# Cross-attention of 20 heads on one Trainium2 core: score tiles of 234, 234 and 156 columns instead of 308, 154 and 154, the second high keys loaded by DMA, and a new order of the batch loop

## Chip, cores and metric

The kernel runs on one core of a Trainium2 chip. The metric is the device time of the program in microseconds (us), the median of several runs; lower is better. The core has a matrix engine (TensorE, in the profile PE, its weight loads PEld), a vector engine (VectorE, DVE), an engine for activations (ScalarE, ACT), a general one (GpSimd, POOL), and SyncE (SP), which here only issues DMA transfers. Each engine works through its own instructions in order; semaphores tie them together.

## The reference, cut to what matters

```
B, S, C = (32, 512, 640); CA = 1024; HEADS = 20; HD = 32     # as drawn
q = heads(x @ to_q_w)                          # 20 heads of 32
k = heads(ctx[:, :77] @ to_k_w)                # 77 text tokens per batch
v = heads(ctx[:, :77] @ to_v_w)
p = softmax(q @ k.T / sqrt(32))                # 77 keys
out = merge(p @ v) @ to_out_w + to_out_b + x
```

The context has 77 tokens, so the three further attentions of the reference (objects, others, images) have no keys and add nothing. All is float32.

## The kernel before

**Numbers in two parts.** Each float32 matrix is split into a high part (`float32r`, the form that TensorE takes) and a low part, the rest. A product is made of three: high by high, high by low, low by high.

**Chunks.** Four heads are 128 rows, so a batch has five chunks; chunk `n` stands for batch `n // 5`, heads `4 * (n % 5)` and on. For each chunk:

- `queries` (line 542, the group pq): 15 products of 512 columns.
- `high_query` (ACT), `copy_query` (POOL, line 783), `low_query` (DVE, line 787) make the three stationary sets `qt[:, 0..2]`: set 0 holds the high query of the four heads; the upper half of set 1 and the lower half of set 2 hold copies of it, the other halves the low query.
- `score_tile` (line 577, the group sc), four tiles of 128 queries: one product of set 0 with the keys of all four heads, 308 = 4 x 77 columns, then one of set 1 with the keys of heads 0 and 1 (154 columns), and one of set 2 with those of heads 2 and 3 (154). A head's 32 rows meet only its own columns, since the key tile is zero elsewhere. A tile stands in one of three PSUM buffers.
- `score_max` (DVE), `exps` (ACT, line 602: four exponentials with their sums), `sums` (DVE, line 612), `normalize` (POOL, line 617), `block_transpose` (DVE), `store_p` (line 633): the weights `pn` go turned to DRAM (`pd<-z`).
- three to four chunks later `load_rows` reads them back (`raw<-pd`, lines 648 and 650), ACT, DVE and POOL split them (`pp`; POOL's part is line 679), and `value_pass` (line 694, pa) makes six products of 512 columns.
- `project` (line 750, po) makes the output: 120 products of 320 columns per batch, then a residual, a bias (POOL, line 743) and a store.

POOL also makes the low part of x (line 320).

**Keys.** They are computed at the start for all batches and stand in DRAM (`k_dram`), high and low. The key tile `kb0` serves chunks 0 to 2, `kb1` chunks 3 and 4. For each batch, `load_keys` brings, per head and group, the high keys to the head's own rows (part 0) and the low keys to another head's rows (part 1), and `copy_half_keys` (POOL, line 519) copies the high keys into the block that set 0 uses.

**The order.** A written table sets the order of everything: each token is one step (`s` score tile, `k` copy of the query, `q` queries, `v` value pass, `p` output product, `d` load of the weights, `w` store of the weights, `uk` load of keys, `K` copy of keys, `N` normalise). `FILL` covers the keys, the values and the first two batches, `PLAN` is one batch and is run 29 times, `LAST_` is the end. A token's place fixes the order on each engine, not its time. SP has one queue for loads and stores; each transfer takes one of eight lanes in turn, and waits for the one before it in its lane.

Of the kernel before, what the change touches and what calls it, by code (L numbers as in the profile page):

```python
# [23 lines left out]
P = 128  # L24
Q = 32
HEADS = 20
HD = 32
# [4 lines left out]
NBLK = HPC * KPAD // Q  # L32

# [18 lines left out]
def kernel(  # L52
# [394 lines left out]
    def open_small():  # L447
        nonlocal small
        if small is None:
# [3 lines left out]
            kbs.append(small.tile([P, 4, GROUPS[0][1], KCOLS // 2], FPR, name="kb0"))  # L453
# [9 lines left out]
    def open_second():  # L463
        nonlocal z
        if not vbs:
# [3 lines left out]
            kbs.append(pool.tile([P, 4, GROUPS[1][1], KCOLS // 2], FPR, name="kb1"))  # L469
# [33 lines left out]
    def load_keys(b, g, heads=range(HPC), parts=(0, 1)):  # L503
        j0, nj = GROUPS[g]
        src = k_dram[g][:, :, :, b * NKEY : (b + 1) * NKEY].bitcast(F32)
        kb = kbs[g].bitcast(F32)
        for i in heads:
            own, half = slice(i * HD, (i + 1) * HD), slice(i % 2 * NKEY, (i % 2 + 1) * NKEY)
            other = slice(*((i + 2) % HPC * HD + k for k in (0, HD)))
            for part, rows in enumerate((own, other)):  # L510
                if part in parts:
                    nc.sync.dma_start(kb[rows, 1 + i // 2, :, half], src[own, part])

    def load_head_keys(b, g, i, part):
        load_keys(b, g, (i,), (part,))

    def copy_half_keys(g, h):
        kb, rows = kbs[g], slice(64 * h, 64 * h + 64)
        nc.gpsimd.tensor_copy(kb[rows, 3 * h], kb[rows, 1 + h].bitcast(F32))

    def copy_keys(g):
        copy_half_keys(g, 0)
        copy_half_keys(g, 1)
# [26 lines left out]
    def split_q(n):  # L550

        qt, pq = qts[n % 2], pqs.pop(n)
        nc.scalar.copy(qt[:, 0, :], pq)
        lower, upper = slice(0, 64), slice(64, P)
        halves = ((lower, upper), (upper, lower))
        for w, (r, other) in enumerate(halves):
            nc.gpsimd.tensor_copy(qt[other, 1 + w, :], qt[r, 0, :].bitcast(F32))
        for w, (r, other) in enumerate(halves):
            nc.vector.tensor_tensor(
                qt[r, 1 + w, :], pq[r], qt[r, 0, :].bitcast(F32), ALU.subtract  # L560
            )

    def score_tile(n, t):
        b, j = divmod(n, NC_)
        g = GROUP_OF[j]
        qt, kb = qts[n % 2], kbs[g]
        jg = j - GROUPS[g][0]
# [560 lines left out]
```

## Time and profile before

| | |
|---|---|
| median of 3 runs | 1858.24 us (1858.23 to 1858.27) |
| profiled execution, its span | 1856.5 us, at clock 1.000 |
| PE busy | 1842.4 us (99%) |
| DVE, ACT, POOL busy | 1563.4, 1527.2, 1303.9 us |
| score products, weight-load rows (line 577) | 1920 in 640 tiles |
| copies of the query on POOL (line 783) | 320, 0.615 us each |
| copies of the keys on POOL (line 519) | 128, 0.443 and 0.576 us |
| loads of keys | 512, 28.9 and 19.2 KB |

How to read it: a busy share is that of the time in which at least one instruction of the engine ran. Matmuls overlap their neighbours, so the length of a row in the timeline is more than what a product adds; the distance from one start to the next is what counts. "idle before" names what ended an engine's idle time. The profile's own time is its span; the median is 1.7 us above it.

### The profile page before, as it was taken

The page shows a single profiled execution, that of the slowest core. Times are in us where ns is not written, and L with a number is a line of the kernel's source. Part 1 is how long each engine was busy: PE and PEld are TensorE (multiplying, and loading weights), DVE is VectorE, ACT ScalarE, POOL GpSimd, SP SyncE. Part 2 cuts the span into 40 slices and gives each one's busy share as a digit, 9 for nine tenths or more (in the row PEclk, how much of TensorE's full clock was granted, in tenths as well). Part 3 has the DMA queues.
Part 4 walks back from the last instruction along what each step waited for, and adds up shares of the span by engine and source line. Part 5 has one row for each costly group of instructions (what it writes and reads, how often), then busy time and mean ns, then how long its engine had stood idle before and what let it go on. Part 6 is the DMA issues. An engine that isn't in the chain of part 4 may idle for free.

```text
span 1856.5 us, 37492 instructions
## 1 busy us (share of the span) xinstructions
PE 1842.4 (99%) x10332; PEld 1655.7 (89%) x10332; DVE 1563.4 (84%) x2502; ACT 1527.2 (82%) x6218; POOL 1303.9 (70%) x1120
## 2 busy tenths in 40 slices
PE   9999999999999999999999999999999999999998
PEld 7888897889999999999999999999999999999998
DVE  5445458899999999999999999999999999999996
ACT  3233248899999999999999999999999999999984
POOL 1100268778788788778778877887778878877874
PEclk9999999999999999999999999999999999999999
DMA  9889779998998898888998888998889988888875
GB/s 188 199 198 249 184 193 256 254 242 235 247 240 243 240 238 232 242 235 236 238 244 237 234 243 237 244 238 237 235 234 244 244 241 236 237 232 243 228 228 187
DMA packets 563296, 431.37 MB, mean 232 GB/s; under 512 B 191120, under 2 KB 471120, under 8 KB 563088
## 3 DMA queue, kind: packets, MB, share of 16 engines
q1 hardware_dynamic: 558192, 413.16, 84.5%
q0 software_dynamic: 4800, 15.65, 2.7%
q8 instruction: 85, 1.39, 0.3%
q14 instruction: 123, 1.01, 0.2%
q10 hardware_dynamic: 96, 0.16, 0.0%
HBM read 247.17 MB, written 181.64 MB: 231 GB/s over the span
## 4 chain that ended last, share of the span: by engine, by line
PE 93%; DMA 4%; SPq 1%; DVE 1%; ACT 1%; issue 0%; POOL 0%; DVEq 0%; ACTq 0%; POOLq 0%
PE po L750 29%; PE pq L542 28%; PE pa L694 12%; PE sc L577 11%; PE pv L204 7%; PE pk L204 6%; DMA pd<-z 1%; DMA cs<-in_ctx_dram 1%; DMA xr<-in_x_dram 1%; DMA wo_s<-wo_dram 0%; DMA wraw<-in_L_xattn_to_v_w_dram 0%; DMA xs<-in_x_dram 0%; DMA wraw<-in_L_xattn_to_k_w_dram 0%; ACT pn L602 0%; DMA raw<-pd 0%
## 5 line engine op out<-in xcount | busy, mean ns | idle before, releaser
L602 ACT ACTIVATE pn<-sc,nm 128x77 f32<-128x77 f32 x2560 | 797.1, 343 | 36.0 <-DVE nm L588 29.6
L750 PE MATMUL po<-wo_s,at 128*128 128x320 f32 x3840 | 707.2, 310 | 0.1
L750 PEld LDWEIGHTS po<-wo_s,at 128*128 128x128 f32 x3840 | 619.7, 188 | 41.1 <-DVE xr L765 0.6
L542 PE MATMUL pq<-xt,wq_s 128*128 128x512 f32 x2400 | 596.7, 394 | 2.9 <-ACT pp L661 1.9
L602 ACT ACTIVATION_READ_ACCUMULATOR pn<-sc,nm 128x1 f32 x2560 | 567.5, 222 | 0.0
L542 PEld LDWEIGHTS pq<-xt,wq_s 128*128 128x128 f32 x2400 | 436.7, 188 | 82.5 <-ACT pp L661 2.1
L617 POOL TENSOR_TENSOR pn<-pn,rs 128x1232 f32<-128x1232 f32 x160 | 389.4, 2434 | 94.0 <-DVE rs L612 90.0
L694 PE MATMUL pa<-pp,vb 128*128 128x512 f32 x960 | 340.9, 403 | 4.1 <-DVE at L731 3.3
L577 PEld LDWEIGHTS sc<-kb,qt 128*128 128x128 f32 x1920 | 302.9, 188 | 14.4 <-ACT pn L602 1.8
L588 DVE TENSOR_REDUCE nm<-sc 128x4 f32<-128x308 f32 x640 | 295.0, 466 | 21.6 <-PE sc L577 16.7
L577 PE MATMUL sc<-kb,qt 128*128 128x154 f32 (+1 forms) x1920 | 301.9, 274 | 0.9 <-ACT pn L602 0.9
L783 POOL CAST qt<-qt 64x512 fp32r<-64x512 f32 x320 | 196.9, 615 | 139.5 <-ACT qt L779 124.4
L712 DVE TENSOR_TENSOR pa<-pa,aw 64x512 f32<-64x512 f32 x320 | 222.3, 695 | 50.4 <-ACT aw L708 43.2
L679 POOL TENSOR_TENSOR pp<-raw,pp 64x512 fp32r<-64x512 f32 x160 | 207.0, 1294 | 66.9 <-ACT pp L661 53.5
L624 DVE STREAM_TRANSPOSE z<-pn 128x1280 f32<-128x1280 f32 x160 | 241.2, 1507 | 8.8 <-DMA pd<-z 3.4
L708 ACT COPY aw<-pa 64x1024 f32<-64x1024 f32 x160 | 162.2, 1014 | 85.0 <-PE pa L694 83.9
L787 DVE TENSOR_TENSOR qt<-pq,qt 64x512 fp32r<-64x512 f32 x320 | 216.8, 678 | 13.9 <-ACT qt L779 9.0
L320 POOL TENSOR_TENSOR xt<-xs,xt 128x512 fp32r<-128x512 f32 x160 | 204.6, 1305 | 20.8 <-ACT xt L316 15.8
L743 POOL TENSOR_TENSOR xr<-xr,bias 128x640 f32<-128x640 f32 x128 | 202.3, 1581 | 13.1 <-issue 3.5
L672 DVE TENSOR_TENSOR pp<-raw,pp 128x1024 fp32r<-128x1024 f32 x160 | 195.7, 1223 | 0.0
L694 PEld LDWEIGHTS pa<-pp,vb 128*128 128x128 f32 x960 | 173.8, 189 | 15.1 <-DVE pp L672 2.3
L663 ACT CAST pp<-raw 128x1024 fp32r<-128x1024 f32 x160 | 168.1, 1051 | 0.7 <-DMA raw<-pd 0.7
(46 smaller groups left out, 1584.2 us busy)
## 6 DMA issues: line engine op xcount, KB each, us to landing
pd<-z SPq DMA_DIRECT2D x640, 160.0 KB, 3.4
raw<-pd SPq DMA_DIRECT2D x160, 512.0 KB, 4.5
xr<-in_x_dram SPq DMA_DIRECT2D x128, 320.0 KB, 3.9
out_dram<-xr SPq DMA_DIRECT2D x127, 320.0 KB, 3.7
xs<-in_x_dram SPq DMA_DIRECT2D x124, 320.0 KB, 5.8
raw<-pd SPq DMA_DIRECT2D x160, 128.0 KB, 4.2
v_dram<-vs SPq DMA_DIRECT2D x80, 192.0 KB, 4.0
k_dram<-ks POOLq DMA_DIRECT2D x20, 512.0 KB, 4.2
```

The costliest lines, as they stand in the source:

```text
L204: nc.tensor.matmul(held[j][:, :gn], w[:, k, a, :], cts[g, k][:, c, :gn], start=(k == 0 and n == 0), stop=(k == NK - 1 and n == 2),)
L542: nc.tensor.matmul(pqs[n], wq_s[:, k, a, j * P : (j + 1) * P], xts[b, k][:, c, :], start=(k == 0 and m == 0), stop=(k == NC_ - 1 and m == 2),)
L577: nc.tensor.matmul(sc[:, cols], qt[:, m, t * P : (t + 1) * P], keys_, start=(m == 0), stop=(m == 2),)
L588: nc.vector.tensor_reduce(nm, sc[:, :KCOLS].rearrange("p (h k) -> p h k", k=NKEY), AX.X, ALU.max, negate=True)
L602: nc.scalar.activation(pnb[n % 2][:, at, :NKEY], sc[:, i * NKEY : (i + 1) * NKEY], AF.Exp, bias=nm[:, i : i + 1], accum_out=sms[n][:, at : ...
L617: nc.gpsimd.tensor_tensor(pf, pf, rs.unsqueeze(2).to_broadcast([P, NQ * HPC, NKEY]), ALU.mult)
L624: nc.vector.transpose(z.rearrange("p b t j -> p t b j"), pn.rearrange("p (t h) k -> p t (h k)", t=NQ).rearrange("p t (b i) -> p t b i", i=Q),)
L679: nc.gpsimd.tensor_tensor(pp[64:, 4, :], raw[:64, 2, :], pp[:64, 4, :].bitcast(F32), ALU.subtract)
L694: nc.tensor.matmul(pas[n][:, p, :], vb[:, p, t, :], pp[:, c, :], start=(c == p), stop=(c == p + 2),)
L712: nc.vector.tensor_tensor(pa[64 * p : 64 * p + 64, 0], pa[:64, p], aw[:, p], ALU.add)
L750: nc.tensor.matmul(pos[b, t, h][:, :HALF], ats[b * NC_ + j][:, a, t * P : (t + 1) * P], wos[0][:, j, c, h * HALF : (h + 1) * HALF], start= ...
L787: nc.vector.tensor_tensor(qt[rows, 1 + w, :], pqs[n][rows], qt[rows, 0, :].bitcast(F32), ALU.subtract)
```

## The change

A head's columns are now 78 wide (`KBLK`, 77 keys and one empty), in the order of heads 2, 0, 1, 3. The twelve products of 32 rows that a tile needs (three parts by four heads) are dealt out over the three stationary sets in another way:

- set 0 (heads 2, 0, 1; 234 columns): high queries of heads 0, 1, 2 and, in the last 32 rows, of head 0 a second time, against its low keys.
- set 1 (heads 0, 1, 3; 234 columns): low queries of heads 0 and 1, high queries of heads 1 and 3.
- set 2 (heads 2, 3; 156 columns, in two pieces of the PSUM tile): high and low queries of heads 2 and 3.

The query needs four copies on POOL instead of two, one of 64 rows and three of 32 (`COPIES`). The last one overwrites head 3's high rows in set 0, so it comes after all that reads them. High keys are needed at two places; the second is loaded from DRAM as part 2 of `load_head_keys`, and the copies on POOL and their token `K` are gone. That is 24 key loads per batch instead of 16. The reduction and the exponentials read the same number of elements, with a step of 78.

`PLAN` is a new order of all steps, not the old one with tokens exchanged. In `FILL` and `LAST_` the old order stands: `k0 k1` where `k0` was, `k2 k3` where `k1` was, part 2 behind part 0, and no `K`.

```diff
+KBLK = NKEY + 1
+ORDER = (2, 0, 1, 3)
+KEYS_AT = (0, 3 * KBLK, 6 * KBLK)
+KEYS_OF = (
+    ((0, 0, 1), (0, 3, 1), (1, 0, 0)),
+    ((0, 1, 2), (1, 2, 1), (1, 1, 1)),
+    ((0, 2, 0), (2, 0, 0), (2, 2, 0)),
+    ((1, 3, 2), (2, 1, 1), (2, 3, 1)),
+)
+COPIES = ((2, 0, 64, 64), (1, 96, 96, 32), (1, 64, 32, 32), (0, 96, 0, 32))
...
-            kbs.append(small.tile([P, 4, GROUPS[0][1], KCOLS // 2], FPR, name="kb0"))
+            kbs.append(small.tile([P, GROUPS[0][1], 8 * KBLK], FPR, name="kb0"))
...
     def load_head_keys(b, g, i, part):
-        load_keys(b, g, (i,), (part,))
-
-    def copy_half_keys(g, h):
-        kb, rows = kbs[g], slice(64 * h, 64 * h + 64)
-        nc.gpsimd.tensor_copy(kb[rows, 3 * h], kb[rows, 1 + h].bitcast(F32))
+        src = k_dram[g][i * HD : (i + 1) * HD, part % 2, :, b * NKEY : (b + 1) * NKEY].bitcast(F32)
+        m, quad, block = KEYS_OF[i][part]
+        c0 = KEYS_AT[m] + block * KBLK
+        nc.sync.dma_start(
+            kbs[g].bitcast(F32)[quad * HD : (quad + 1) * HD, :, c0 : c0 + NKEY], src
+        )
...
+    def score_blocks(sc):
+        return sc[:, : HPC * KBLK].rearrange("p (h k) -> p h k", k=KBLK)
+
     def score_tile(n, t):
...
-        half = KCOLS // 2
-        for m, (cols, keys_) in enumerate(
-            (
-                (slice(0, KCOLS), kb[:, 0::3, jg]),
-                (slice(0, half), kb[:, 1, jg]),
-                (slice(half, KCOLS), kb[:, 2, jg]),
-            )
-        ):
+        blocks = score_blocks(sc)
+        for m, heads in enumerate((blocks[:, 0:3], blocks[:, 1:4], blocks[:, 0::3])):
+            nh = (3, 3, 2)[m]
+            keys_ = kb[:, KEYS_AT[m] : KEYS_AT[m] + nh * KBLK].rearrange("p (h k) -> p h k", k=KBLK)
             nc.tensor.matmul(
-                sc[:, cols],
+                heads,
                 qt[:, m, t * P : (t + 1) * P],
                 keys_,
                 start=(m == 0),
                 stop=(m == 2),
+                skip_group_check=True,
             )
...
     def copy_query(n, w):
-        qt, half = qts[n % 2], (slice(0, 64), slice(64, P))
-        nc.gpsimd.tensor_copy(qt[half[1 - w], 1 + w, :], qt[half[w], 0, :].bitcast(F32))
+        qt, (m, r1, r0, rn) = qts[n % 2], COPIES[w]
+        nc.gpsimd.tensor_copy(qt[r1 : r1 + rn, m, :], qt[r0 : r0 + rn, 0, :].bitcast(F32))
...
     PLAN = (
-        "1uv10 0r 0e0 0s2 0ux3 0g0 0N 0v0 1uv15 0v1 0m1 0v2 0f10 0p16 1uv11 0e1 0v4 0g1 0uk120 0p17 0v3 "
+        "1uv13 0uk121 0m1 0e0 0v1 0k0 0g1 0s2 0p16 0v3 0uk122 0f10 0ux3 0v0 0v5 0e1 0v2 0m2 0v4 0r 0uk111 "
...
-        elif op == "K":
-            copy_half_keys(*arg)
```

**Where instructions move.** On TensorE, in the loop, two score tiles of one chunk (sc, output from PSUM's three tiles; kb is the key tile, qt the query) between query (pq), output (po) and value (pa) products. Before:

```order
L694 MATMUL pa<-pp,vb_2005 128x512
L750 MATMUL po<-wo_s,at_2689 128x320 x3
L577 MATMUL sc<-kb_1753,qt_1920 128x308
L577 MATMUL sc<-kb_1753,qt_1920 128x154 x2
L577 MATMUL sc<-kb_1753,qt_1920 128x308
L577 MATMUL sc<-kb_1753,qt_1920 128x154 x2
L542 MATMUL pq<-xt,wq_s 128x512 x15
```

and after the change:

```order
L538 MATMUL pq<-xt,wq_s 128x512 x9
L726 MATMUL po<-wo_s,at_2715 128x320 x3
L558 MATMUL sc<-kb_2007,qt_1923 128x234 x2
L558 MATMUL sc<-kb_2007,qt_1923 128x2x78
L558 MATMUL sc<-kb_2007,qt_1923 128x234 x2
L558 MATMUL sc<-kb_2007,qt_1923 128x2x78
L726 MATMUL po<-wo_s,at_2379 128x320 x3
L670 MATMUL pa<-pp,vb_2009 128x512 x6
```

A tile has three products as before, the longest is shorter, and the two others of 154 are one of 234 and one of two pieces of 78; query products are now cut up between output products.

On POOL, in the loop, the stretch from the normalisation (pn) ahead of the query's copies (qt) for chunk 3 to the copies for chunk 4; pp is POOL's part of the weights, xt the low part of x, xr the bias. Before:

```order
L617 TENSOR_TENSOR pn_1922<-pn_1922,rs 128x16x77
L783 CAST qt_1920<-qt_1920 64x512 x2
L679 TENSOR_TENSOR pp<-raw,pp 64x512
L743 TENSOR_TENSOR xr<-xr,bias 128x640
L617 TENSOR_TENSOR pn_1921<-pn_1921,rs 128x16x77
L679 TENSOR_TENSOR pp<-raw,pp 64x512
L320 TENSOR_TENSOR xt<-xs,xt 128x512
L783 CAST qt_1919<-qt_1919 64x512 x2
L320 TENSOR_TENSOR xt<-xs,xt 128x512 x4
```

and after the change:

```order
L593 TENSOR_TENSOR pn_1924<-pn_1924,rs 128x16x77
L759 CAST qt_1922<-qt_1922 64x512
L759 CAST qt_1922<-qt_1922 32x512 x3
L330 TENSOR_TENSOR xt<-xs,xt 128x512
L719 TENSOR_TENSOR xr<-xr,bias 128x640
L593 TENSOR_TENSOR pn_1925<-pn_1925,rs 128x16x77
L655 TENSOR_TENSOR pp<-raw,pp 64x512
L330 TENSOR_TENSOR xt<-xs,xt 128x512 x4
L759 CAST qt_1923<-qt_1923 64x512
L759 CAST qt_1923<-qt_1923 32x512 x3
```

Two copies became four, and those for chunk 4 moved behind the four splits of x.

On SP, in the loop, stores of the weights (pd) and the load of earlier weights (raw) that follows them, each with what it waits for (DMAHW is one of the eight lanes). Before:

```order
L633 DMA pd<-z 32x10x128 [waits DMAHW4_49,DVE_49]
L512 DMA kb_1753<-k_dram_60 32x3x77 [waits DMAHW5_49]
L633 DMA pd<-z 32x10x128 [waits DMAHW6_49]
L633 DMA pd<-z 32x10x128 [waits DMAHW7_49]
L633 DMA pd<-z 32x10x128 [waits DMAHW0_49]
L739 DMA xr<-in_x_dram 128x640 [waits DMAHW1_49]
L302 DMA xs<-in_x_dram 32x16x160 [waits DMAHW2_49,Pool_49]
L650 DMA raw<-pd 64x512 [waits DMAHW3_49]
L648 DMA raw<-pd 128x2x512 [waits DMAHW4_49,DMAHW0_49,DMAHW6_49,DVE_49,DMAHW7_49,Activation_49,Pool_49]
```

and after the change:

```order
L609 DMA pd<-z 32x10x128 [waits DMAHW7_49,DVE_49]
L609 DMA pd<-z 32x10x128 [waits DMAHW0_49]
L609 DMA pd<-z 32x10x128 [waits DMAHW1_49]
L527 DMA vb_2009<-v_dram 32x3x96 [waits DMAHW2_49]
L624 DMA raw<-pd 128x2x512 [waits DMAHW3_49]
L517 DMA kb_1753<-k_dram_60 32x3x77 [waits DMAHW4_49]
L609 DMA pd<-z 32x10x128 [waits DMAHW5_49]
L517 DMA kb_1753<-k_dram_60 32x3x77 [waits DMAHW6_49]
L312 DMA xs<-in_x_dram 32x16x160 [waits DMAHW7_49,Pool_49]
```

The load of weights waited for the four stores just ahead of it; now it waits for its lane only.

More of the change, by code (lines that the diff above doesn't have):

```diff
@@ L468, in open_second @@
             pool = ctx.enter_context(tc.tile_pool(name="second", bufs=1, reuse_waits="tile"))
-            kbs.append(pool.tile([P, 4, GROUPS[1][1], KCOLS // 2], FPR, name="kb1"))
+            kbs.append(pool.tile([P, GROUPS[1][1], 8 * KBLK], FPR, name="kb1"))
             z = pool.tile([P, NBLK, NQ, Q], F32, name="z")
@@ L548, in queries @@
                 )
[L550 to L560, printed above, removed]
-            )
+    def score_blocks(sc):
+        return sc[:, : HPC * KBLK].rearrange("p (h k) -> p h k", k=KBLK)
     def score_tile(n, t):
@@ L599, in exps @@
             sms[n] = small.tile([P, NQ * HPC], F32, tag="sm", name="sm", bufs=2)
-        for i in range(HPC):
-            at = t * HPC + i
+        for i, head in enumerate(ORDER):
+            at = t * HPC + head
             nc.scalar.activation(
                 pnb[n % 2][:, at, :NKEY],
-                sc[:, i * NKEY : (i + 1) * NKEY],
+                sc[:, i * KBLK : i * KBLK + NKEY],
                 AF.Exp,
```

24 lines of the change are left out of this document (2 added, 22 removed), and 167 rows, old and new, of tables (FILL, LAST_, PLAN).

## The prediction

> **What bounds the kernel now.** I read the page first (span, busy shares, chain), then the stretches, then TensorE's own rows in order of time, then the waits.
>
> ```profile
> span 1856.5 us, 37492 instructions
> PE 1842.4 (99%) x10332; PEld 1655.7 (89%) x10332; DVE 1563.4 (84%) x2502; ACT 1527.2 (82%) x6218; POOL 1303.9 (70%) x1120
> PE 93%; DMA 4%; SPq 1%; DVE 1%; ACT 1%; issue 0%; POOL 0%; DVEq 0%; ACTq 0%; POOLq 0%
> ...
> core 0: us, PE busy (x) PEld busy (x) DVE busy (x) ACT busy (x) POOL busy (x), PEclk, DMA share, GB/s
> 1000.00:1200.00 200.00, 200.00 (x1168) 182.19 (x1167) 183.20 (x296) 185.01 (x784) 161.01 (x136) 1.00 0.89 240
> ```
>
> TensorE (PE) makes 93% of the chain that ended last, and in the stretch from 1000 to 1200 us it has no idle time at all, at the full clock. ACT stands at 93%, DVE at 92%, POOL at 81% and the DMA engines at 89%. So TensorE sets the time, and the others have room of 7 to 19%. A busy PE says nothing on what its products cost, so I read the distances between their starts (columns: start, length, group, count):
>
> ```profile
> 1002.73 0.49 PE L577 MATMUL sc<-kb,qt 128*128 128x308 f32 x3
> 1003.05 0.44 PE L694 MATMUL pa<-pp,vb 128*128 128x512 f32 x1
> 1003.33 0.60 PE L750 MATMUL po<-wo_s,at 128*128 128x320 f32 x3
> 1003.77 0.39 PE L694 MATMUL pa<-pp,vb 128*128 128x512 f32 x1
> 1004.00 1.04 PE L750 MATMUL po<-wo_s,at 128*128 128x320 f32 x6
> 1004.88 0.49 PE L577 MATMUL sc<-kb,qt 128*128 128x308 f32 x3
> ...
> 1005.91 0.86 PE L577 MATMUL sc<-kb,qt 128*128 128x308 f32 x6
> 1006.61 3.65 PE L542 MATMUL pq<-xt,wq_s 128*128 128x512 f32 x15
> 1010.10 0.60 PE L750 MATMUL po<-wo_s,at 128*128 128x320 f32 x3
> ...
> 1055.60 3.65 PE L542 MATMUL pq<-xt,wq_s 128*128 128x512 f32 x15
> ...
> 1002.50 0.57 PEld L577 LDWEIGHTS sc<-kb,qt 128*128 128x128 f32 x3
> 1002.98 0.19 PEld L694 LDWEIGHTS pa<-pp,vb 128*128 128x128 f32 x1
> 1003.09 0.58 PEld L750 LDWEIGHTS po<-wo_s,at 128*128 128x128 f32 x3
> ```
>
> Six output products (320 columns) go from 1004.00 to 1004.88: 0.147 us each. A value product (512) takes 0.23 (1003.77 to 1004.00), and so does a query product (3.49/15). That is a line of 0.083 us over 192 columns, 0.43 ns a column. A score tile is 308+154+154 columns. With the value product behind it, it takes 0.60 (1002.73 to 1003.33), so 0.37 alone. On the line it would be 0.142 + 0.075 + 0.075 = 0.29. The weight rows say why it isn't: the loads around the tile's end start at 1002.50 + 0.57 - 0.19 = 1002.88, 1002.98 and 1003.09, 0.10 to 0.11 us apart, although each product has to have its own. **A product with fewer columns than take 0.11 us costs 0.11 us**, because the next load isn't ready: 0.142 + 0.11 + 0.11 = 0.362, as measured. (The stamps show only 0.32 from the tile to the next product; the delay is in the product behind it, 0.28 instead of 0.23.)
>
> The batch closes the account. The same place returns after 1055.60 - 1006.61 = 48.99 us, with 75 query, 30 value and 120 output products and 20 tiles in it. Without the 0.04 that hangs over from the tile a query product is 3.45/15 = 0.23: 17.25 + 6.90 + 17.64 = 41.79 us, and what is left is 7.20, 0.360 a tile. Between this and 0.37 I take 0.365. So a batch holds no other lost time.
>
> **The change, part by part.**
>
> *Columns.* Each tile is now 234, 234 and 156 columns, 624 instead of 616. By the line a product of 234 columns takes 0.147 - 86 x 0.00043 = 0.110 us; that is just the distance of the weight loads. The third has 156 columns and costs the 0.11 of the load behind it. The tile costs three times 0.110 to 0.112, 0.330 to 0.336; I take 0.333. No 234-column product is in the trace; the 308-column one (which also reads its keys in two blocks) and the 154-column one stand on both sides, and both fit. Gain per tile 0.365 - 0.333 = 0.032, bounds 0.360 - 0.336 = 0.024 and 0.370 - 0.330 = 0.040: over the 640 tiles of the run **20.5 us** (15 to 26).
>
> *Key loads and key copies.* Per batch 8 more loads on SP, and 4 POOL casts gone.
>
> ```profile
> L519 POOL CAST kb<-kb 64x462 fp32r<-64x462 f32 x64 | 36.8, 576 | 4.9 <-DMA kb<-k_dram 1.2
> L519 POOL CAST kb<-kb 64x308 fp32r<-64x308 f32 x64 | 28.3, 443 | 6.7 <-DMA kb<-k_dram 3.1
> L783 POOL CAST qt<-qt 64x512 fp32r<-64x512 f32 x320 | 196.9, 615 | 139.5 <-ACT qt L779 124.4
> L679 POOL TENSOR_TENSOR pp<-raw,pp 64x512 fp32r<-64x512 f32 x160 | 207.0, 1294 | 66.9 <-ACT pp L661 53.5 <-DMA xr<-in_x_dram 5.4 <-POOL xr L743 0.7
> L320 POOL TENSOR_TENSOR xt<-xs,xt 128x512 fp32r<-128x512 f32 x160 | 204.6, 1305 | 20.8 <-ACT xt L316 15.8 <-POOL pp L679 0.3
> ...
> DMA packets 563296, 431.37 MB, mean 232 GB/s; under 512 B 191120, under 2 KB 471120, under 8 KB 563088
> ...
> kb<-k_dram SPq DMA_DIRECT2D x256, 28.9 KB, 3.0
> kb<-k_dram SPq DMA_DIRECT2D x256, 19.2 KB, 3.2
> ...
> L512 SPq DMA_DIRECT2D kb<-k_dram x360: 302/447/2686, 600.1 to 1698.1; - x180
> ```
>
> The 512 key loads carry 12.3 MB; half as many again is 6.2 MB, 1.4% of all bytes, and 256 x 80 rows = 20480 packets, 3.6% of all packets. DMA share 0.89 becomes 0.90 to 0.92: not full, and on no path of TensorE's while loads come early. SP issues 8 x 0.447 = 3.6 us more per batch. Cost taken: nothing; cover: the distance between a key load and its first score tile (rival 3 has the price if it is gone).
>
> *Query copies.* Two casts of 64 rows per chunk become one of 64 and three of 32. No 32-row cast is in the trace. On POOL 64 rows (1294 ns) and 128 rows (1305 ns) of 512 cost the same, so I take 615 ns for 32 rows too (lower bound: half). POOL gets 2 x 0.615 x 5 = 6.15 us a batch and loses 2 x (0.576 + 0.443) = 2.04: 39.4 (0.805 of 48.99) becomes 43.5 of 48.35 us, 90%. It fits, but its order has little room. The last copy overwrites rows 96 to 127 of the high query, so it also waits for the second DVE subtraction and the copy that read them. Queued behind it on POOL are the normalisations and the splits of x; the first score tile of the chunk waits for it. In the present loop the room there is small (below it the rows that price POOL's and the DVE's longest piece):
>
> ```profile
> 1042.37 1.28 POOL L783 CAST qt<-qt 64x512 fp32r<-64x512 f32 x2
> ...
> 1044.13 0.49 PE L577 MATMUL sc<-kb,qt 128*128 128x308 f32 x3
> ...
> L617 POOL TENSOR_TENSOR pn<-pn,rs 128x1232 f32<-128x1232 f32 x160 | 389.4, 2434 | 94.0 <-DVE rs L612 90.0 <-DMA pd<-z 3.5
> L743 POOL TENSOR_TENSOR xr<-xr,bias 128x640 f32<-128x640 f32 x128 | 202.3, 1581 | 13.1 <-issue 3.5 <-DMA xr<-in_x_dram 1.3 <-DMA pd<-z 1.0
> L765 DVE TENSOR_TENSOR xr<-po,xr 128x320 f32<-128x320 f32 x256 | 121.0, 474 | 14.0 <-PE po L750 13.8
> L306 DVE STREAM_TRANSPOSE xs<-xs 128x640 f32<-128x640 f32 x128 | 104.4, 819 | 0.6 <-DMA xs<-in_x_dram 0.6
> L612 DVE RECIPROCAL rs<-sm 128x16 f32<-128x16 f32 x160 | 39.8, 249 | 7.2 <-ACT pn L602 4.4
> ```
>
> The copies end at 1043.65, the tile starts at 1044.13: 0.48 us. Two more casts would not fit in that. But the loop's order is new as well. For the tightest chunk the order put 12 output and 6 value products and 1 tile between the last query product and the first tile, 12 x 0.147 + 6 x 0.23 + 0.367 = 3.5 us; now it is 24 output, 15 query and 6 value products and 4 tiles: 3.5 + 3.4 + 1.4 + 1.3 = 9.7. All five chunks now have 8.1 to 9.8 us (before 3.5 to 9.0). POOL's longest dense piece, the one shown of its order: normalise 2.43, 4 copies 2.46, one x split 1.31, bias 1.58, normalise 2.43, values 1.29, 4 x splits 5.22, 4 copies 2.46, together 19.2 us. From the output product that frees the DVE ahead of its reciprocal to the score tile that needs the last copies TensorE has 45 query, 60 output and 12 value products and 8 tiles, 10.3 + 8.8 + 2.8 + 2.7 = 24.6 us. The DVE's piece between (adding that product, a transpose of x, the reciprocal) is 0.47 + 0.82 + 0.25 = 1.54. It fits, with 3.9 us for queues ahead. Cost taken in the loop: nothing.
>
> *Loop order, loads and stores.* The rows that the words of the change speak of:
>
> ```profile
> SPq L633 <- DMA xs<-in_x_dram: 28.4, 25, 1.4
> SPq L648 <- DMA pd<-z: 22.4, 42, 1.4
> ```
>
> From 600 to 1700 us SP waited 22.4 us for stores of the weights ahead of the loads that read them back, 1 us a batch. TensorE did not wait for it, so ending it buys nothing by itself; it makes room for the 3.6 us of new issues.
>
> *Start and end.* The tables of the first two batches and the last one keep their order and get the two casts right at the old places. There the room is partly nil:
>
> ```profile
> 339.90 0.61 POOL L783 CAST qt<-qt 64x512 fp32r<-64x512 f32 x1
> 340.51 0.87 PE L577 MATMUL sc<-kb,qt 128*128 128x308 f32 x6
> ...
> 1790.88 1.64 POOL L783 CAST qt<-qt 64x512 fp32r<-64x512 f32 x1
> ```
>
> Per chunk 1.23 us more and 0.41 less (a key cast gone): 0.82, against room of 0 to 3.5. For 15 chunks that is 0 to 12 us; since a delay at one chunk gives the next ones room, I take **4 us**.
>
> **Sum.** 1856.5 - 20.5 + 4 = 1840.0 us of span. The timed runs are 1.7 us above the span (1858.24), so **1842 us**; with the bounds 1833 to 1855.
>
> **The rivals.**
>
> 1. *POOL becomes the bound (slower).* The fourth copy is late in every batch, at the chunks that had least room. Price: 0.82 - 0.48 = 0.34 us at two of five chunks, 64 x 0.34 = 22 us: 1842 + 22 = 1864; at all 160 chunks 1842 + 54 = 1896. It decides from 0.13 us a chunk (20.5/160). For it: POOL at 90%, in-order, with spans that vary (the cast of 1.64 us above). Against: 8 us and more of TensorE work now lie ahead of every first tile. Chance 0.11.
>
> 2. *A tile costs its columns.* If the short products were not held by the weight loads, 624 columns for 616 would add 8 x 0.43 ns x 640 = 2.2 us: 1860. The rows (0.37 against 0.29) speak against it: chance 0.01. Nearer is that the change doesn't do what it says, and a 234-column product costs 0.12 or more: the tile 0.36, the gain 0.005 x 640 = 3 us, less the 4: 1859. Against: the line through 154 (0.075, hidden under the loads) and 308. Chance 0.04. The Trainium skill, "TensorE: Matmul & The Clock Gate", section "Back-to-back issue gap", gives the single matmul as N/2.4 + 2.5 ns; by that a tile goes from 264 to 267.5 ns and the change loses 2 us. By that rule no gain is possible; the trace disagrees (0.37 us for a tile), and the same section says that the formula leaves out the weight loads.
>
> 3. *Key loads come too late.* A key load takes 3.0 to 3.2 us to land, and SP stands behind loads of x (28.4 us of waits). If the last of a group is late by 0.3 us once a batch, 30 x 0.3 = 9 us: 1851; at 0.5 us 1857. For it: 24 key loads instead of 16 in one queue. Against: no wait of PE for a DMA in the loop now. Chance 0.10.
>
> **How the numbers follow.** Forecast 0.74 (own range 1836 to 1850), rivals 0.11, 0.05 (both halves) and 0.10. About 0.2% (3.7 us) is what can be told from no change. Faster: 0.74 + 0.07 of rival 3 = 0.81. Same: the rest of 3 and rival 2, 0.08. Slower: 0.11. The range, 1836 to 1854, takes the forecast's own and the first half of rival 3.
>
> **What would show it.** Right: the place in the loop returns after 48.3 to 48.4 us, a tile with a value product behind it takes 0.56 to 0.57 instead of 0.60, PE stays without idle time, POOL's share is near 0.90 and the DMA's 0.90 to 0.92. Wrong: waits of PE for POOL's copies (rival 1) or for key loads (rival 3) in the loop, or a tile that still takes 0.36 or more (rival 2). A start that is longer by over 12 us would break the fourth term.

## The result and the profile after

The changed kernel takes **1923.84 us** (median of 4 runs, 1919.94 to 1925.89); the kernel before, on the same chip, 1858.26. The ratio is **1.0349** (95% interval 1.0335 to 1.0364): 3.5% slower, where 0.9% faster was forecast.

First the page of the changed kernel (span, busy shares, chain):

```profile
span 1922.1 us, 37554 instructions
PE 1872.4 (97%) x10332; PEld 1639.2 (85%) x10332; DVE 1605.8 (84%) x2502; ACT 1546.5 (80%) x6218; POOL 1530.1 (80%) x1312
...
PE 29%; POOL 19%; ACT 13%; DVE 12%; DMA 6%; SPq 5%; issue 4%; POOLq 0%; DVEq 0%; ACTq 0%
```

and its stretch from 1000 to 1200 us (busy time and instructions of PE, PEld, DVE, ACT and POOL, then clock, DMA share, GB/s):

```profile
1000.00:1200.00 200.00, 196.75 (x1124) 173.27 (x1123) 182.82 (x284) 180.93 (x746) 183.43 (x153) 1.00 0.90 233
```

TensorE had 93% of the chain that ended last; now it has 29%, and POOL, ACT and DVE take turns in the rest. TensorE has idle time in the loop (196.75 of 200), at the same clock. POOL went from 161 to 183 us in this stretch.

The same place in the loop now returns after 1066.59 - 1015.85 = 50.74 us, not 48.99 (PE's rows in order of time; the last one's bracket says what it waited for):

```profile
1015.85 0.79 PE L558 MATMUL sc<-kb,qt 128*128 128x234 f32 x5 [0.29 <-POOL qt L759]
...
1066.59 0.79 PE L558 MATMUL sc<-kb,qt 128*128 128x234 f32 x5 [0.29 <-POOL qt L759]
```

Below, "the loop" is a mean over 25 batches: from the first score tile of the fifth batch to that of the thirtieth, divided by 25. It is 48.99 us before and 50.83 after. The 65.6 us between the spans lie in three places: 12.6 up to the first tile of the fourth batch (401.3 against 413.9), 47.7 in the 26 batches behind it, 5.3 after that. One batch of the loop (1.8) is in the first and two are in the last, so the start lost 10.8 and the end 1.6.

The waits from 600 to 1800 us show that no single one makes up the loss. They are small, on every engine, and most are there one to three times a batch (23.6 batches lie in this window; columns: waits in us, times, longest):

```profile
ACT pn L578 <- DVE nm L570: 60.0, 72, 1.5
DVE nm L570 <- PE sc L558: 33.5, 48, 0.9
...
PEld sc L558 <- POOL qt L759: 21.2, 48, 0.5
...
PE pa L670 <- DVE at L707: 11.3, 24, 0.7
```

What changed on POOL and the DVE is the length of single instructions. The page's groups (busy, mean ns of one, idle time before):

```profile
L759 POOL CAST qt<-qt 32x512 fp32r<-32x512 f32 (+1 forms) x640 | 470.1, 734 | 53.5 <-ACT qt L755 11.8
L655 POOL TENSOR_TENSOR pp<-raw,pp 64x512 fp32r<-64x512 f32 x160 | 245.8, 1536 | 64.7 <-ACT pp L637 42.7
L648 DVE TENSOR_TENSOR pp<-raw,pp 128x1024 fp32r<-128x1024 f32 x160 | 236.8, 1480 | 2.9 <-ACT pp L639 0.3
```

and POOL's and the DVE's rows in order of time:

```profile
1053.33 2.31 POOL L593 TENSOR_TENSOR pn<-pn,rs 128x1232 f32<-128x1232 f32 x1
1055.71 2.13 POOL L655 TENSOR_TENSOR pp<-raw,pp 64x512 fp32r<-64x512 f32 x1
1063.03 3.51 POOL L759 CAST qt<-qt 64x512 fp32r<-64x512 f32 x4
...
1054.32 2.40 DVE L648 TENSOR_TENSOR pp<-raw,pp 128x1024 fp32r<-128x1024 f32 x1
1064.08 1.31 DVE L648 TENSOR_TENSOR pp<-raw,pp 128x1024 fp32r<-128x1024 f32 x1
```

A copy takes 734 ns in the mean instead of 615, POOL's subtraction 1536 instead of 1294. The rows in order of time show why. The DVE's subtraction of the weights (L648, two operands in SBUF) starts at 1054.32, while POOL's normalise runs until 1055.64; it ends at 1056.72, 1.08 us after the normalise. POOL's own subtraction starts at 1055.71, inside it, and takes 2.13 us; it ends 1.12 us after the DVE's has ended. (Undisturbed, the two take some 1.2 and 1.29 us.) At 1064.08 the DVE's subtraction starts ahead of POOL's third copy, and that copy alone takes 1.49 us; the four copies take 3.51 us instead of 4 x 0.61. **Whichever starts first is undisturbed; the other gets almost nothing done until it ends.** That is theory A of the experiments: POOL and this subtraction take turns, so the five subtractions of 1.2 us a batch come on top of POOL's work.

### The profile page after: what moved, and what is told of

It reads as the page before. It is cut to its first block, busy times and chain, and to the rows that moved or that the text cites. A ratio compares the mean times of both kernels' runs of the same rounds, so it can differ in the third digit from the quotient of the medians.

```text
span 1922.1 us, 37554 instructions
## 1 busy us (share of the span) xinstructions
PE 1872.4 (97%) x10332; PEld 1639.2 (85%) x10332; DVE 1605.8 (84%) x2502; ACT 1546.5 (80%) x6218; POOL 1530.1 (80%) x1312
## 4 chain that ended last, share of the span: by engine, by line
PE 29%; POOL 19%; ACT 13%; DVE 12%; DMA 6%; SPq 5%; issue 4%; POOLq 0%; DVEq 0%; ACTq 0%
PE po L726 10%; PE pq L538 9%; ACT pn L578 9%; POOL xt L330 7%; POOL qt L759 6%; PE sc L558 4%; PE pa L670 4%; POOL pn L593 3%; DVE pp L648 3%; DVE nm L570 2%; POOL pp L655 2%; SPq L609 2%; ACT pp L639 2%; DMA pd<-z 2%; DVE xs L316 2%
## 5 line engine op out<-in xcount | busy, mean ns | idle before, releaser
L726 PEld LDWEIGHTS po<-wo_s,at 128*128 128x128 f32 x3840 | 608.4, 189 | 43.3 <-DMA wo_s<-wo_dram 1.0
L538 PE MATMUL pq<-xt,wq_s 128*128 128x512 f32 x2400 | 634.7, 396 | 3.0 <-DVE qt L763 1.5
L578 ACT ACTIVATION_READ_ACCUMULATOR pn<-sc,nm 128x1 f32 x2560 | 547.0, 214 | 0.0
L759 POOL CAST qt<-qt 32x512 fp32r<-32x512 f32 (+1 forms) x640 | 470.1, 734 | 53.5 <-ACT qt L755 11.8
L593 POOL TENSOR_TENSOR pn<-pn,rs 128x1232 f32<-128x1232 f32 x160 | 368.0, 2300 | 29.7 <-DVE rs L588 24.5
L558 PEld LDWEIGHTS sc<-kb,qt 128*128 128x128 f32 x1920 | 283.6, 190 | 67.4 <-POOL qt L759 34.1
L570 DVE TENSOR_REDUCE nm<-sc 128x4 f32<-128x308 f32 x640 | 288.8, 463 | 58.6 <-PE sc L558 48.8
L670 PE MATMUL pa<-pp,vb 128*128 128x512 f32 x960 | 309.7, 406 | 22.4 <-DVE at L707 16.7
L558 PE MATMUL sc<-kb,qt 128*128 128x234 f32 (+1 forms) x1920 | 295.2, 271 | 16.2 <-POOL qt L759 13.7
L655 POOL TENSOR_TENSOR pp<-raw,pp 64x512 fp32r<-64x512 f32 x160 | 245.8, 1536 | 64.7 <-ACT pp L637 42.7
L648 DVE TENSOR_TENSOR pp<-raw,pp 128x1024 fp32r<-128x1024 f32 x160 | 236.8, 1480 | 2.9 <-ACT pp L639 0.3
```

Source lines behind the costliest of these rows:

```text
L538: nc.tensor.matmul(pqs[n], wq_s[:, k, a, j * P : (j + 1) * P], xts[b, k][:, c, :], start=(k == 0 and m == 0), stop=(k == NC_ - 1 and m == 2),)
L558: nc.tensor.matmul(heads, qt[:, m, t * P : (t + 1) * P], keys_, start=(m == 0), stop=(m == 2), skip_group_check=True,)
L570: nc.vector.tensor_reduce(nm, score_blocks(sc)[:, :, :NKEY], AX.X, ALU.max, negate=True)
L578: nc.scalar.activation(pnb[n % 2][:, at, :NKEY], sc[:, i * KBLK : i * KBLK + NKEY], AF.Exp, bias=nm[:, i : i + 1], accum_out=sms[n][:, at ...
L593: nc.gpsimd.tensor_tensor(pf, pf, rs.unsqueeze(2).to_broadcast([P, NQ * HPC, NKEY]), ALU.mult)
L648: nc.vector.tensor_tensor(pp[:, 2:4, :], raw[:, 0:2, :], pp[:, 0:2, :].bitcast(F32), ALU.subtract)
```

## The experiments

| kernel | time us | ratio to before (95%) | loop us |
|---|---|---|---|
| before | 1858.3 | 1 | 48.99 |
| changed | 1923.8 | 1.0349 (1.0335 to 1.0364) | 50.83 |
| e1 one operand | 1907.2 | 1.0265 (1.0244 to 1.0287) | 50.32 |
| e2 old order | 1965.4 | 1.0572 (1.0552 to 1.0592) | 52.32 |
| e3 new order alone | 2100.3 | 1.1289 (1.1253 to 1.1325) | 57.20 |
| e4 short copies | 1917.8 | 1.0315 (1.0294 to 1.0337) | 50.57 |
| e7 fewer key loads | 1918.1 | 1.0321 (1.0306 to 1.0337) | 50.77 |
| e8 short copies, fewer loads | 1888.6 | 1.0160 (1.0145 to 1.0175) | 49.78 |
| e9 copy by ACT | 1914.2 | 1.0295 (1.0280 to 1.0311) | 50.47 |
| e10 old order, mended | 1956.9 | 1.0523 (1.0505 to 1.0540) | 51.99 |
| e11 one operand, fewer loads | 1862.1 | 1.0019 (1.0009 to 1.0028) | 48.73 |
| e12 one operand, thin loads | 1879.8 | 1.0111 (1.0078 to 1.0145) | 49.15 |
| e13 before, more starts | 1936.5 | 1.0426 (1.0393 to 1.0458) | 51.47 |
| e14 before, double copies | 1981.1 | 1.0655 (1.0637 to 1.0673) | 52.94 |
| e15 start, short copies | 1862.2 | 1.0016 (1.0006 to 1.0025) | 48.73 |
| e16 start, fewer loads | 1857.7 | 0.9996 (0.9987 to 1.0005) | 48.77 |
| e17 start, both | 1855.3 | 0.9976 (0.9966 to 0.9986) | 48.73 |
| e18 before, one operand | 1857.6 | 0.9994 (0.9984 to 1.0003) | 48.99 |

**e1: POOL and DVE freed of each other.**

```diff
-        nc.vector.tensor_tensor(
-            pp[:, 2:4, :], raw[:, 0:2, :], pp[:, 0:2, :].bitcast(F32), ALU.subtract
-        )
+        nc.vector.tensor_reduce(
+            pp[:, 2:4, :].rearrange("p k q -> p (k q)"),
+            raw[:, 0:2, :].rearrange("p k (q o) -> p (k q) o", o=1), AX.X, ALU.max
+        )
```

> The changed kernel in which the DVE's subtraction of the weights (L648, two operands in SBUF) is a reduction over groups of one element of the same 128x1024 with one operand in SBUF; the low part of the weights is left out with it. Theory A (POOL and that subtraction take turns, so that five times 1.2 us a batch are lost to POOL): POOL's copies are all back at 0.6 us and its normalise at 2.3 us, the loop returns after 48.3 to 48.6 us and the time is 1842 to 1862 us. Theory B (POOL is late because four copies depend on each other and on ACT, whatever the DVE does): the copies keep their mean of 730 to 780 ns, the loop stays at 50.7 us and the time at 1915 to 1925 us. Theory C (the new order of the loop costs the time): as B.

Groups of e1 by shape, 600 to 1800 us:

```profile
L760 POOL CAST qt<-qt 32x512 fp32r<-32x512 f32 x360 | 219.9, 611 | 38.5 <-DVE qt L764 17.9
L656 POOL TENSOR_TENSOR pp<-raw,pp 64x512 fp32r<-64x512 f32 x119 | 153.0, 1286 | 50.3 <-ACT pp L637 42.8
L760 POOL CAST qt<-qt 64x512 fp32r<-64x512 f32 x120 | 73.1, 609 | 13.5 <-ACT qt L756 7.7 <-DMA out_dram<-xr 0.3
L648 DVE TENSOR_REDUCE pp<-raw 128x1024 fp32r<-128x1024 f32 x119 | 141.3, 1187 | 0.0
```

The turn-taking is shown: with one operand of the DVE's instruction in SBUF, of the same size and length (1187 ns), every copy is back at 0.61 us and POOL's subtraction at 1.29. But the time only fell to 1907, half a microsecond a batch. A is real and not the whole; something else holds the loop at 50.3, now irregularly (48.8 to 51.9 from batch to batch). (The edit also frees the DVE of its wait for ACT's cast, but that wait was 0.3 us in the whole run.) Among the waits that were not in the changed kernel are these for transfers:

```profile
POOL xr L720 <- DMA xr<-in_x_dram: 15.2, 15, 1.7
DVE z L600 <- DMA pd<-z: 15.0, 21, 2.2
...
ACT pp L637 <- DMA raw<-pd: 12.1, 8, 2.6
...
PE sc L558 <- DMA kb<-k_dram: 6.6, 6, 2.0
```

**e2 and e3: the order.** Both were badly made. e2 puts the tokens of before's order into the changed kernel, e3 the other way round:

```diff
 e2, order:  - 3k1 ... 3g0 ... 3k0 ... 3g1      + 3k0 3k1 ... 3g0 ... 3k2 3k3 ... 3g1
 e3, order:  - 0k2, 0k3, 0uk120 0uk122, ...     + 0uk120 1K11, 0uk100 2K10, 3uk010 3K00, 3uk020 4K01
```

> The changed kernel with the loop order of the kernel before: its first copy of each chunk has become the first two copies and its second the last two, the second high keys are loaded right behind the first, and POOL's key copies are gone. Theory A: POOL has the same work, so the loop stays between 50.2 and 51.5 us and the time at 1905 to 1945 us. Theory C (the new order): the loop goes to 48.3 to 48.9 us and the time to 1842 to 1865 us. Theory B: as A.

> The kernel before with the loop order of the change alone: two copies a chunk at the places of the first two of the four, POOL's key copies behind the loads that they need, no second high keys by DMA. Theory A: POOL has 45 us of work with the subtraction in a loop of 49 us, so the loop stays within 48.7 to 49.5 us and the time at 1850 to 1880 us. Theory C: the loop is 50.3 to 51 us and the time 1905 to 1930 us. Theory B: as A.

In e2 the copy over rows 96 to 127 came ahead of the subtraction that reads them in two of five chunks, so the low part of one head's queries came out changed and the subtraction waited. In e3 I had put POOL's key copies right behind the loads they need, and POOL, which works in order, stood still until those landed (the granted clock fell to 0.96 in that run). The first row is e2's, the second e3's, 600 to 1800 us:

```profile
DVE qt L763 <- POOL qt L759: 43.1, 46, 1.7
```

```profile
POOL kb L519 <- DMA kb<-k_dram: 264.7, 62, 6.9
```

Neither says anything on the order; e10 mends e2. The new order on the old kernel stays untried in a fair form.

**e4: three of four copies shortened.**

```diff
+        s = slice(0, 32 if w and n > 2 * NC_ else S)
-        nc.gpsimd.tensor_copy(qt[r1 : r1 + rn, m, :], qt[r0 : r0 + rn, 0, :].bitcast(F32))
+        nc.gpsimd.tensor_copy(qt[r1 : r1 + rn, m, s], qt[r0 : r0 + rn, 0, s].bitcast(F32))
```

> The changed kernel in which the three 32-row copies of the query move 32 of their 512 columns from the third batch on; the rest of the query's second and third copy is then stale. The copies stay as instructions at their places and fall from 0.6 to about 0.15 us. Theory A and B: POOL loses about 7 us a batch, the loop returns after 48.3 to 48.6 us and the time is 1842 to 1862 us, which also says what the smaller tile is worth alone; A expects the copies that are left to be stretched still, mean of the 64-row copy above 700 ns, without a cost. Theory C: the loop stays above 50 us and the time above 1900 us.

1917.8 us, with POOL's busy time in the window down from 1099.6 to 950.9 us. A and B missed: POOL's work alone isn't the limit. The numbers are those that C gives, the order of the loop, which stays a rival up to e10 and e11. The other candidate is the issuing engine SP: it was busy for 36.4 us a batch before and 41.6 after, without the gaps between its instructions. That gave theory D.

**e7 and e8: the second high keys not loaded in the loop.**

```diff
 PLAN: - 0uk122 0uk112 0uk102 3uk032 3uk012 3uk002 3uk022 5uk132
```

> The changed kernel without the eight loads a batch of the second high keys from the third batch on; the products then read old keys there. New theory D: with POOL relieved the loop had still stayed at 50.3 us, and SP, which starts every load and store in order, was busy for 41.5 us and 4.2 us of gaps between starts out of 50.7 (36.3 and 3.7 out of 49.0 before the change): SP's eight more starts make loads and stores late. D alone (POOL is no limit): SP loses 4.3 us a batch, the loop goes to 48.3 to 49.0 us, the time to 1842 to 1865 us. D beside A (each is enough to hold the loop): the loop stays at 50.1 to 50.7 us and the time is 1905 to 1922 us. C (the order): as D beside A.

> The two cuts together: the three 32-row copies of the query move 32 columns, and the second high keys are not loaded from the third batch on. A and D together account for the loss: the loop returns after 48.3 to 48.7 us and the time is 1842 to 1865 us. C (the order of the loop costs it by itself): the loop stays above 49.8 us and the time above 1890 us.

e7 alone gives nothing (50.77 for 50.83 us), as if D were wrong. With e4's cut it gives 0.8 us a batch (49.78 for 50.57). That speaks for **two limits side by side, of which each hides the other**. e8 ended between the two expectations; in it the DVE's subtraction still takes 1503 ns in the mean, so A is only weakened by short copies. POOL is busy for only 964 of 1200 us there.

**e9: one copy given to ACT.** Nothing is left out here.

```diff
         nc.scalar.copy(qts[n % 2][:, 0, :], pqs[n])
+        m, r1, r0, rn = COPIES[1]
+        nc.scalar.copy(qts[n % 2][r1 : r1 + rn, m, :], pqs[n][r0 : r0 + rn])
...
     def copy_query(n, w):
+        if w == 1:
+            return
```

> The changed kernel in which the copy of the fourth head's high query is made by ACT out of PSUM, right behind its cast of the whole query, and not by POOL; the values are the same. POOL loses 5 copies of 0.6 us, ACT gains 5 of about 0.5 us. A alone: POOL's work with the subtraction is 45.6 us, the loop goes to 48.4 to 49.0 us and the time to 1845 to 1870 us. A beside D, or C: as with the short copies, the loop stays at 50.1 to 50.6 us and the time at 1908 to 1922 us.

1914.2 us and a steady 50.5: as forecast for two limits (C forecast the same). ACT is now busy for 1163 of 1200 us, so it has little room left.

**e10: before's order, mended.**

```diff
 e2's order, with each k3 behind that chunk's g0 and g1
```

> The changed kernel with the loop order of the kernel before, in which the copy over the last 32 rows now stands behind both subtractions that read those rows, so that the subtractions wait for no copy: first and second copy at the old place of the first, third at that of the second. C: the loop goes to 48.3 to 49.2 us and the time to 1842 to 1875 us. A and D: the work of POOL and SP is the same as in the changed kernel, so the loop is 50.0 to 51.5 us and the time 1900 to 1945 us.

1956.9 us, slower than every theory said. The old order lets the scores wait for four copies in a row, on the weight loads and on the products (600 to 1800 us):

```profile
PEld sc L558 <- POOL qt L759: 52.8, 47, 1.2
PE sc L558 <- POOL qt L759: 39.2, 47, 0.9
```

So the new order did not cost the time: with the new products it is worth 33 us against the old one as e10 fills it.

**e11: e1 and e7 together.** The test of A and D.

> The one-operand kernel (the DVE's subtraction of the weights is a reduction with one operand in SBUF, so POOL and DVE no longer take turns; the low part of the weights is left out) also without the loads of the second high keys from the third batch on. The short copies with fewer loads had left a loop of 49.63 us, in which the DVE's subtraction still took 1.50 us for 1.20. A and D together are the whole loss in the loop: 48.3 to 48.8 us, time 1845 to 1865 us (the start keeps its 9 to 13 us). The order of the loop costs something by itself (C), or the four copies in a row do (B): the loop stays at 49.3 to 50.4 us, the time at 1875 to 1908 us.

Its stretch from 600 to 1800 us:

```profile
600.00:1800.00 1200.00, 1198.67 (x7009) 1081.55 (x7009) 1099.86 (x1771) 1123.32 (x4679) 1046.26 (x959) 1.00 0.91 239
```

TensorE is busy for 1198.67 of 1200 us, and the loop is 48.73. The four cells of the loop are now full: both limits 50.83, turn-taking alone (e7) 50.77, loads alone (e1) 50.32, neither 48.73. Each alone costs 1.6 to 2.0 us a batch; together they cost 2.1. Order and length of the chain of copies (C and B of the expectations) cost the changed loop nothing that is left to see. Set beside e8, this also says what the turns cost: e8 has the same loads, and POOL busy for 40.0 us a batch, so that even with five subtractions of 1.2 us there is room in its sum; yet its loop is 1.05 us longer. So it is not POOL's sum alone that costs; that single instructions that come late hold up the others is likely, and not shown.

**e12: are the loads dear as starts or as transfers?**

```diff
+        if part == 2 and b > 2:
+            nc.sync.dma_start(kbs[g].bitcast(F32)[quad * HD : quad * HD + 2, :, c0 : c0 + NKEY], src[:2])
```

> The one-operand kernel, in which each load of the second high keys moves 2 of its 32 rows from the fourth batch on: SP makes as many starts, the DMA engines have a sixteenth of that work. D is SP's starts: loop as in the one-operand kernel (a mean of 50.4 us, irregular), time 1900 to 1912 us. D is the transfers: as in the kernel without those loads, whatever that shows, and at least 0.7 us a batch below 50.4.

With all 24 starts and a sixteenth of the additional transfers the loop is 49.15 us, between the two expectations: of the 1.59 us between e1 and e11, 1.17 went with the size of the loads, and 0.42 stays. So the number of starts, theory D's first form, is the smaller part. But a thin load's start is shorter too (600 to 1800 us; least, median and greatest ns; L518 the thin loads, L520 the others):

```profile
L520 SPq DMA_DIRECT2D kb<-k_dram x391: 302/428/1792, 601.4 to 1797.0; - x196
L518 SPq DMA_DIRECT2D kb<-k_dram x197: 234/294/739, 600.6 to 1796.7; - x197
```

SP's busy time fell from 42.7 to 40.3 us a batch, by more than the loop. So e12 does not tell whether the loads cost as SP's time or as time of the DMA engines.

**e13 and e14: each limit put into the kernel before.**

```diff
 e13 (behind each load of a high key, from the fourth batch on):
+        nc.sync.dma_start(spare.bitcast(F32)[rows, :, half], src[own, part, :2])
 e14:
         nc.gpsimd.tensor_copy(qt[half[1 - w], 1 + w, :], qt[half[w], 0, :].bitcast(F32))
+        nc.gpsimd.tensor_copy(qt[half[1 - w], 1 + w, :], qt[half[w], 0, :].bitcast(F32))
```

> The kernel before with eight more key loads a batch from the fourth batch on: each load of a high key is made a second time, two of its chunks, into a tile that nothing reads. SP goes from 40.0 to about 44.4 us of 49.0. D in its strong form (SP's starts hold any loop of this kind): the loop goes to 49.5 to 51 us, the time to 1873 to 1915 us. D in its weak form (SP matters in the order that was written for a shorter loop): within 49.0 to 49.4 us, 1856 to 1870 us. A alone: no change, 1856 to 1861 us.

> The kernel before with each of its two query copies made twice, the second time over the first: POOL's work goes from 39.3 us a batch to 45.4, with the subtraction's 6.0 us in the way to 51.4, in a loop of 49.0; SP, keys and order are those of before. A: the loop goes to 51.4 us or a little more, the time to 1920 to 1975 us, and the scores wait for POOL. If POOL's turn-taking is no limit: the loop stays under 49.6 us and the time under 1880 us.

Eight loads a batch whose data no engine waits for cost the kernel before 77 us over the 29 batches that have them, with its old order, products and POOL work; D's strong form had said 15 to 57. The stretch of e13 from 600 to 1800 us (PE's busy time first, the DMA share before the last):

```profile
600.00:1800.00 1200.00, 1163.74 (x6634) 1040.60 (x6633) 1052.09 (x1675) 1055.19 (x4422) 915.40 (x768) 1.00 0.89 231
```

TensorE is idle for 36 of 1200 us, and the DMA share is 0.89, as it was before. **No run here had a share above 0.91; here more transfers made the loop longer, not the share higher.** That the DMA engines were full is not shown by it: SP was busy for 42.0 us a batch (before 36.4) and waited only 2.4 for other engines (before 7.2), so its queue had little room left either. Which of the two holds the loop stays open. e14 went to 52.94 us with the DMA's work unchanged, 1.5 beyond A's 51.4; the scores wait for POOL there (46.2 us on the weight loads), so its cost is POOL's work and the chain of copies together.

**e15 to e17: the start.** Made from e11.

```diff
 e15: - 32 if w and n > 2 * NC_ else S          + 32 if w and 2 <= n <= 2 * NC_ else S
 e16: 17 of the tokens for second high keys out of the first two batches' table
```

> The one-operand kernel with fewer loads, in which also in the first two batches (from the third chunk on) the three 32-row copies move 32 columns. The start: from the first score tile to that of the eleventh chunk the kernel before takes 94.6 us, the changed one 103.6 and the kernel this is made from 107.0. Theory S1 (the start loses to the scores' wait for four copies in a row): 95 to 100 us, time 1850 to 1856 us. Theory S2 (it loses to the additional key loads): 104 to 108 us, time 1858 to 1866 us.

> The one-operand kernel with fewer loads, in which 17 loads of second high keys in the first two batches are left out too, and the copies are whole. S1: from the first score tile to that of the eleventh chunk 104 to 108 us, time 1858 to 1866 us. S2: 95 to 100 us, time 1850 to 1856 us.

> Both cuts of the start together. If S1 and S2 are its whole loss: from the first score tile to that of the eleventh chunk 92 to 95 us (94.6 in the kernel before, less some 3 us for 120 smaller tiles), time 1844 to 1852 us. If the order written for the loop's first chunks loses too: more than 98 us and a time above 1853 us.

From the first score tile to that of the eleventh chunk: before 94.6 us, changed 103.6, e11 107.1, e15 103.8, e16 97.2, e17 96.1. This stretch varies, though: the changed kernel, e2, e7 and e10 have the same instructions in it, and took 103.1 to 107.2 us. So e15 shows no gain from the copies alone, and e16 one of 6 to 10 us from the loads. The ratios of the table, from 8 to 10 runs each, give 0.23% (4 us) for the loads, nothing clear of noise for the copies alone, and 0.43% (8 us) for both: here too the copies count once the loads are out. S1 fell, though the waits of the changed kernel there (258 to 362 us) name the copies first:

```profile
PEld sc L558 <- POOL qt L759: 6.7, 6, 2.1
PEld pa L670 <- ACT pp L639: 3.4, 2, 2.2
```

My reading, which no run shows, is that the view names a copy that was late because its own inputs were late, and not the transfer at the root. e17 is the change with both of its costs taken out: 1855.3 us, 0.24% below before, and short of the 1844 to 1852 expected. (That expectation counted 120 smaller tiles in the stretch; there are 40, worth 1 us and not 3.)

**e18: the turns before the change.** e1's edit in the kernel before.

> The kernel before with the DVE's subtraction of the weights made a reduction with one operand in SBUF (the low part of the weights is left out). A: before the change POOL and the subtraction fit beside each other, only the normalise was stretched; its mean falls from 2434 to 2280 ns and the subtraction's stays at 1.19 us; the loop stays at 48.99 us and the time within 1855 to 1860 us. If the turns had cost the kernel before something too: the loop falls below 48.8 us and the time below 1853 us.

POOL's normalise in it, 600 to 1800 us:

```profile
L617 POOL TENSOR_TENSOR pn<-pn,rs 128x1232 f32<-128x1232 f32 x123 | 280.0, 2277 | 66.8 <-DVE rs L612 63.2 <-DMA pd<-z 3.6
```

The normalise fell from 2434 to 2277 ns, the loop stayed at 48.99. The turns were there before, in one instruction a batch, and cost nothing.

No run of these beats the kernel before with the whole computation: the nearest of the changed ones that leaves nothing out is e9, at 1.0295.

## Why the prediction was wrong

*Columns* (a gain of 20.5 us): right in kind, too large. Three products of the tile stand 0.108 to 0.112, 0.112 and 0.075 us apart, the last with its delay in the product behind, as the prediction had it. A tile with a value product behind it takes 0.571 us (median), inside the 0.56 to 0.57 that was named; but before it took 0.596, not 0.60. That is 0.025 for 0.032, 0.5 us a batch. And of that only 0.26 reached the loop, in e11, where nothing else is lost (48.99 to 48.73). By the distances between starts from 700 to 1700 us, the score products fell from 6.64 to 6.16 us a batch and the value products from 7.23 to 7.06, while the 75 query products rose from 17.34 to 17.55 (231.2 to 234.0 ns each) and the output products from 17.79 to 17.96. For the query products the new order is part of it: it cuts them into 289 runs in that window instead of 142. Late in the long runs of before they stood 227 ns apart (median), in the short ones of now 228 to 233, and 235 ahead of an output product. Why is open, and so is the rest. The term measured 0.26 x 32 = 8 us.

*Key loads and key copies* (nothing): the first step that failed. The cover that was named, the time between a key load and its tile, did hold in the changed kernel: key loads land 3.9 us after their start, and PE didn't wait for them (only with the turns gone, in e1, did it wait, 6.6 us in 1200). What was lost was time of the other transfers. The prediction read a DMA share of 0.89 as room, and put 3.6 us on SP, where 5.2 were measured (36.4 to 41.6 us a batch). e13 shows that eight more loads a batch lengthen even the old loop, and e1 against e11 that they cost 1.6 us a batch when nothing hides them. Whether it is SP's queue or the DMA engines that had no room stays open. Rival 3 had the right place, 24 loads in one queue, but priced it on the key loads' first tile, and not on the residual rows, the stores and the weights in the same queue (the waits of e1).

*Query copies* ("It fits, but its order has little room"; nothing): the second step that failed. 615 ns for 32 rows was right to 4 ns (611 in e1). What failed is "it fits": 43.5 us of POOL's work for 48.35 left out that POOL and the DVE's subtraction stand still for each other. With 5 x 1.2 us it is 49.5, more than the forecast loop of 48.35 (48.7, if the normalise is taken at its undisturbed 2.28), so no room was left for anything that comes late. The turns alone then cost 2.0 us a batch (e7 against e11). That the sum by itself gives this price is not shown: in the changed kernel POOL was busy for 46.6 us of 50.83, held-up instructions included, and in e8, with room in the sum, 1.05 us were still lost. The row was in the prediction: a normalise of 2434 ns, whose undisturbed length is 2277 (e18). Its mean was taken as its price, without the spread behind it. The Trainium skill, "SBUF — State Buffer", section "Who interferes with whom", states the rule: a DVE instruction with two inputs in SBUF contends with a GpSimd instruction that reads SBUF, the one that starts first holds the ports for its whole length, and a reduction on trn2 never contends. The rows agree in each point: 2.13 and 2.40 us for instructions of 1.29 and 1.2 that started second, and all back at their lengths in e1. Rival 1 said "POOL becomes the bound" at 1864 to 1896 and named the copies as the place. Place and sign were right, and the price, 0.34 us a chunk, is near the 0.41 of the turns (2.04 / 5), but by luck: it came from the length of the chain of copies, which e11 shows to cost nothing. It was given too little, 0.11, because the 19.2 us piece was added up from means, without the turns. Rival 2 fell with the tile's 0.571. Two signs that were named for a right forecast came about without it: POOL's share was 0.92 and the DMA's 0.90 in a loop that waits.

*Loop order, loads and stores* (nothing by itself): the order had to be there. Without it the new products lose 33 us more (e10).

*Start and end* (4 us): measured 10.8 and 1.6. The prediction gave the copies as the cause; e16 shows that the loads, which it had priced at nothing there as well, are a large part, and that the copies gain anything shows only with the loads out as well (e15, e17).

*The sum*: 1842 forecast, 1923.8 measured. With the two costs taken out, e17 gives 1855.3; so some 68 us are turns and key loads, and some 13 us are a smaller gain and what is left in the start.

## What to carry to other kernels

Before work is moved to POOL, add to POOL's busy time every DVE instruction with two SBUF operands, and compare that sum with the loop, as a first check; look at the spread of an instruction's durations, not at its mean. A DMA share of 0.9 may be all that a pattern gives, and the engine that starts the transfers may be as full: add a few transfers that nobody waits for and see whether the loop grows. When undoing one suspect changes nothing, undo two at once: two limits of nearly the same length hide each other, and here undoing one gave 0.1 (loads) or 0.5 us a batch (turns), undoing both 2.1.

## What the runs showed of the hardware

- POOL's instructions on SBUF and the DVE's 128x1024 subtraction of two SBUF operands nearly exclude each other, for the whole instruction: a four-copy piece of 2.44 us took 3.51, a subtraction of 1.2 us took 2.40. A reduction of the same 128x1024 with one SBUF operand (1187 ns) left POOL alone.
- POOL's cast costs the same for 32 and for 64 rows of 512 (611 and 609 ns). 32 rows of 32 columns took 340 ns in the mean in e4, still with disturbed ones among them (median 206 in e8).
- A start on SP was shorter for a smaller load: 294 ns (median) for two rows, 428 for 32 (e12).
- Eight more loads a batch, 1.1% more bytes over the run in e13 (417.75 MB for 413.16 in the main queue), made a loop of 49 us 2.5 us longer, at an unchanged DMA share.
